# ConvNeXt block and Mamba block on one core: the down projection and the input projection put behind a sum on TensorE, and the depthwise convolution's parts put into other steps

## The chip, the cores and the metric

The kernel runs on one core of a Trainium2 chip. The metric is the device time of one execution in microseconds (us), taken as the median of several runs. A profile is one further execution, recorded instruction by instruction. Its engines are PE (TensorE, matrix products; PEld are its weight loads), DVE (VectorE), ACT (ScalarE), POOL (GpSimd) and SP, which only issues DMAs here.

## The reference

The input is 32 images of 96 channels and 56 x 56 pixels, in float32. Two layers follow each other.

Layer 0 is a ConvNeXt block: a depthwise 7 x 7 convolution, a norm over the channels, an up projection from 96 to 384 channels with Gelu, a down projection back to 96, and the residual.

Layer 1 takes the 3136 pixels of an image as a sequence and runs two Mamba blocks over it. Cut to what matters:

```python
xs, z = split(norm(seq) @ in_w)                 # 96 -> 2 x 192
xc = silu(conv4(xs) + conv_b)                   # causal, four taps
dt, Bm, Cm = split(xc @ xproj_w)                # 6, 16 and 16 columns
delta = softplus(dt @ dt_w + dt_b)              # 192
h[t] = exp(delta * A) * h[t-1] + delta * Bm * xc    # 192 x 16 states
y = (sum over the 16 states of h * Cm) + Dp * xc
seq = seq + (y * silu(z)) @ out_w
```

Then come a 1 x 1 fusion with a vector pooled from the layer's input, a batch norm over all images, and a residual.

## The kernel before, in words

**Stages.** One stage is one Mamba layer i of one image b for one quarter c of its sequence (784 positions, held as two halves of 392). There are 2 x 32 x 4 = 256 stages, listed in `order`, with layer 0 and layer 1 of the block alternating and a layer-1 stage standing two places behind the layer-0 stage of the same quarter. A stage has 24 steps: six groups j of 32 channels, times four groups g of four states. In each step `scan` runs one scan of 128 rows x 784 positions on VectorE (L885); the decay comes from ScalarE's exponential (`exps`, L836), and GpSimd multiplies the result by Cm (L889).

**The input of a scan.** For four of the six groups j, TensorE spreads u = delta * xc over the 128 rows (`spread`, L851, two matmuls into a "wide" PSUM tile of which there are two), and VectorE multiplies by Bm (L878) ahead of the scan. For the groups in `POOLED` (steps 8 to 11 and 20 to 23) GpSimd makes that product (L862), and the exponential goes into a wide tile. So a spread is issued in the steps 3, 11, 15 and 23, for the product that follows in step 4, 12, 16 and in step 0 of the next stage.

**The sums.** `add_up(n - 3)` in step n sums over the states with matmuls (L921) into the tile y, for odd j, behind a first matmul with D (L914) for g = 0. "The sums of step 15" are thus issued in step 18. `gate` (L903, VectorE) multiplies y by silu(z); there are three gates in a stage, in the steps 4 and 12 and behind the scan of step 19. The one behind step 19 reads the sums of steps 12 to 15.

**What lies between.** All other work is cut into pieces with a slot number. The whole part is the step (a negative number, or one over 24, lies in the stage before or after), the fraction orders the pieces of a step. In each step the order on every engine is: exponentials for later steps, the scan, the spread, the gate behind step 19, `add_up`, and then the pieces of that step.

- `prep`, for the stage that comes next: load, norm (`center` L355, `square` L360, `mean` L365, `root` L371), the input projection (`project`, L587: three blocks q of 64 columns with four taps, each in two pieces, into the PSUM tile of that q, then the z part), `silu` (L600), `dbl` (L614), `dt` (L644, 6 rows, all three PSUM tiles), `softplus` (L652), and the loads of Bm, Cm (`load_bc`), delta (`load_d4`) and u (`load_u`). The times t of the projection pieces apply to all stages but three special ones.
- `post`, for the stage that just ended: `project` at 7.5 (L750, L756), `move` at 9 and 10, and for layer 1 the statistics and the store.
- `block0`: half a quarter of the ConvNeXt block of the next image: norm, `up` (L424, the three PSUM tiles), `gelu` (L432), `down` (L439 and L443, PSUM tile 2), `residual` (L450, and a store on SP). At the end of an image come `total` (VectorE), `pool` (L464 on TensorE, Relu L466 on ScalarE) and `fuse` (L470, L472), both through PSUM tile 2.
- `conv`: the depthwise convolution of two channels for seven images, one per stage in the stages 2 to 145, as band matrices. Part 0 has four images, part 1 three; each has seven taps (L506, one matmul each), accumulated in PSUM tile 2, and a `store` (L519 on ScalarE, then a DMA). The band and the padded input are loaded at -1.

**Order on an engine.** The main part is under a manual schedule: each engine runs its instructions in the order of the program, and waits at the first that isn't ready. The PSUM tiles 0, 1 and 2 exist once each:

```python
return pp.tile([128, 512], F32, name="ps", tag=f"ps{k}", bufs=1)
```

so a piece that writes one of them waits until the last reader of what was in it is through. For each tile these readers are ScalarE or VectorE instructions.

Of the kernel before, what the change touches and what calls it, by code (L numbers as in the profile page):

```python
# [51 lines left out]
NCH = 4  # L52
# [9 lines left out]
def convnext_mamba_kernel(  # L62
# [185 lines left out]
    for k in range(2):  # L248
        t = const.tile([C + 1, 3 + CH], F32, name=f"hn{k}", tag=f"hn{k}")
        nc.vector.memset(t[C : C + 1, :], 1.0)  # L250
        hns.append(t)
        t = const.tile([C + 1, HC], F32, name=f"hz{k}", tag=f"hz{k}")
# [7 lines left out]
    with tc.tile_pool(name="cc", bufs=1) as cc, tc.tile_pool(name="cx", bufs=3) as cx, tc.tile_pool(  # L260
# [32 lines left out]
        for i in range(3):  # L293
            t = cc.tile([R2, 7, R2], F32, name=f"band{i}", tag=f"band{i}")
            nc.gpsimd.memset(t, 0.0)
            bands.append(t)
            t = cc.tile([R2, b0, W + 6], F32, name=f"xpad{i}", tag=f"xpad{i}")
# [31 lines left out]
    with ExitStack() as main:  # L329
# [23 lines left out]
        def centred(src, k):  # L353
            ps = psum(k)
            nc.tensor.matmul(ps[0:C, 0:HC], center_m, src, start=True, stop=True)  # L355
            return ps

        def squared(ps):
            sq = wp.tile([R2, HC], F32, name="sq", tag="sq", bufs=3)[0:C]
            nc.scalar.activation(sq, ps[0:C, 0:HC], AF.Square)  # L360
            return sq

        def mean_of(sq, k):
            ps = psum(k)
            nc.tensor.matmul(ps[0:C, 0:HC], mean_m, sq, start=True, stop=True)  # L365
            return ps

        def rsqrt(ps):

            rs = ps[0:C, 0:HC]  # L370
            nc.scalar.activation(rs, rs, AF.Ln, bias=eps_c[0:C])  # L371
            nc.scalar.activation(rs, rs, AF.Exp, scale=-0.5)
# [10 lines left out]
        def block0(b, c, s):  # L383
            k = c * 2 + s
            v = {}

            def load():
                if k == 0:
                    batch_sums[b] = wp.tile([C, NCH * 2], F32, name="sums", tag="sums", bufs=2)
                v["cv"] = wp.tile([C, ROWS, W], F32, name="cv", tag="cv", bufs=1)  # L390
                g = 0 if b < b0 else 1 + (b - b0) // NB
                at = (b - groups[g][0]) * W
                nc.sync.dma_start(
                    v["cv"],
                    conv_d[g].rearrange("(c h) w -> c h w", h=H)[
                        :, k * ROWS : (k + 1) * ROWS, at : at + W
                    ],
                )

            def load_x():  # L400
                if s == 0:
                    xins[b, c] = wp.tile([C, CH], F32, name="xin", tag="xin", bufs=1)
                    nc.sync.dma_start(xins[b, c], x[b, :, c * CH : (c + 1) * CH])

            def center():
                v["cv"] = v["cv"].rearrange("p r w -> p (r w)")
                v["ps"] = centred(v["cv"], 2)

            def square():
                v["sq"] = squared(v["ps"])  # L410

            def mean():
                v["ps"] = mean_of(v["sq"], 2)

            def root():
                rsqrt(v["ps"])

            def norm():
                nc.vector.tensor_tensor(hn0s[s][0:C], v["cv"], v["ps"][0:C, 0:HC], ALU.mult)

            def up():
                v["pss"] = [psum(f) for f in range(NF)]
                for f in range(NF):
                    nc.tensor.matmul(  # L424
                        v["pss"][f][:, 0:HC], w1_sb[:, f * 128 : (f + 1) * 128], hn0s[s],
                        start=True, stop=True,
                    )

            def gelu():
                v["gl"] = wp.tile([128, NF, HC], F32, name="gl", tag="gl", bufs=1)  # L430
                for f in range(NF):
                    nc.scalar.activation(  # L432
                        v["gl"][:, f], v["pss"][f][:, 0:HC], AF.Gelu, bias=b1_sb[:, f : f + 1]
                    )
                exp_ln_tables()

            def down():
                v["ps"] = psum(2)
                nc.tensor.matmul(  # L439
                    v["ps"][0:C, 0:HC], eye, xins[b, c][:, tok(s)], start=True, stop=False  # L440
                )
                for f in range(NF):
                    nc.tensor.matmul(  # L443
                        v["ps"][0:C, 0:HC], w2_sb[:, f, :], v["gl"][:, f, :],
                        start=False, stop=(f == NF - 1),
                    )

            def residual():
                xs = xins[b, c][:, tok(s)]
                nc.scalar.activation(  # L450
                    xs, v["ps"][0:C, 0:HC], AF.Identity, bias=b2ls,
                    accum_out=batch_sums[b][:, k : k + 1],
                )
                if s == 1:
                    nc.sync.dma_start(x1_d[b][:, c * CH : (c + 1) * CH], xins.pop((b, c)))


            def total():
                v["m"] = wp.tile([C, 1], F32, name="mean", tag="gps")
                nc.vector.tensor_reduce(v["m"], batch_sums[b], AX.X, ALU.add)  # L460

            def pool():
                ps = psum(2)
                nc.tensor.matmul(ps[0:C, 0:1], gpw_sb, v["m"], start=True, stop=True)  # L464
                v["gp"] = wp.tile([C, 1], F32, name="gp", tag="gps")
                nc.scalar.activation(v["gp"], ps[0:C, 0:1], AF.Relu, bias=gpb, scale=1.0 / L)  # L466

            def fuse():
                ps = psum(2)
                nc.tensor.matmul(ps[0:C, 0:1], fw2, v["gp"], start=True, stop=True)  # L470
                fb = wp.tile([C, 1], F32, name="fb", tag="fb", bufs=3)
                nc.scalar.activation(fb, ps[0:C, 0:1], AF.Identity, bias=fusb)  # L472
                batch_bias[b] = fb

            last = [(21.5, total), (29.9, pool), (30.9, fuse)] if k == 2 * NCH - 1 else []
            return last + [
                (-6, load), (2, load_x), (11.3, center), (12.1, square), (12.4, mean),
                (12.8, root), (14.1, True, norm), (15.6, up), (15.9, gelu), (17.3, down),
                (18.3, residual),
            ]  # L480


# [5 lines left out]
        def conv(g, p):  # L488
            lo, hi = groups[g]
            v = {}  # L490

            def load():
                v["band"] = wp.tile([R2, 7, R2], F32, name="band", tag="band", bufs=1)
                nc.sync.dma_start(v["band"].rearrange("p k n -> p (k n)"), band_d[p])
                nc.sync.dma_start(
                    xpad[:, :, 3 : 3 + W],
                    x[lo:hi, 2 * p : 2 * p + 2, :].rearrange("b c (h w) -> (c h) b w", w=W),
                )

            def tap(part, dw):  # L500
                first, last = PARTS[part]

                def piece():
                    if dw == 0:
                        v["ps"] = psum(2)
                    nc.tensor.matmul(  # L506
                        v["ps"][0:R2, 0 : (last - first) * W], v["band"][:, dw, :],
                        xpad[:, first:last, dw : dw + W], start=(dw == 0), stop=(dw == 6),
                    )

                return piece

            def store(part):
                first, last = PARTS[part]
                n = (last - first) * W

                def piece():
                    t = wp.tile([R2, HC], F32, name="sq", tag="sq", bufs=3)
                    nc.scalar.activation(  # L519
                        t[:, 0:n], v["ps"][0:R2, 0:n], AF.Identity, bias=cb[:, p : p + 1]  # L520
                    )
                    nc.sync.dma_start(
                        conv_d[g][p * R2 : (p + 1) * R2, first * W : last * W], t[:, 0:n]
                    )

                return piece

            at = (7.7, 8.2, 8.6, 9.2, 9.6, 10.2, 10.4), (18.5, 18.6, 19.2, 20.2, 21.2, 21.3, 22.2)
            return [
                (-1, load), (11.05, store(0)), (22.9, store(1)),  # L530
                *[(at[part][dw], tap(part, dw)) for part in range(2) for dw in range(7)],
            ]

# [7 lines left out]
        def prep(S):  # L541
# [164 lines left out]
                (-18, load), (-12.9, center), (-11.9, square), (-11.8, halo), (-11.6, mean),  # L706
                (-11.2, root), (-9, True, norm),
            ]
            t = (-7.6, -7.5, -6.5, -6, 0, 0.1, 1, 2.3, 3.1, 3.4, 4)
            if S in (stages[2], stages[-1]):  # L710

                start = [
# [3 lines left out]
                t = (12, 12, 13, 13, 14, 14, 15, 16, 17, 18, 19)  # L716
            elif S is stages[3]:
# [5 lines left out]
                t = (0, 0, 0.1, 0.2, 0.3, 1, 2, 3.3, 4.1, 4.4, 5)  # L723
            t = [k + 0.1 for k in t]
# [362 lines left out]
```

## Time and profile before

| what | value |
|---|---|
| median of 3 runs | 17,911.81 us (17,886.25 to 17,983.38) |
| the profiled execution | 17,900.79 us |
| its span from the first to the last instruction | 17,899.1 us |
| ahead of the first scan / from the last scan on | 639 us / 371 us |
| mean granted clock of TensorE | 0.851 |
| busy: VectorE, GpSimd, TensorE, ScalarE | 90%, 87%, 82%, 64% |
| TensorE's wait for VectorE's scans ahead of a spread (L851) | 2109.8 us |
| moved by DMA | 2346 MB, 131 GB/s |

Times in the table are from the runs and from the page of the profile. A row of the timeline or of the groups has, in this order, the start where it is a timeline, the time that the instructions took together, the engine, the line of the kernel, the operation, what it writes and reads, the shape (for matmuls rows x columns of the weights, then the moving operand) and the count; in brackets stand the idle time of the engine before it and who ended that. A row of waits has the waiting instruction, the one waited for, the time in total, how often, and the longest. A float32 matmul of the program stands as two instructions in the counts of TensorE.

### The profile page before, as it was taken

The numbers are of one execution on the slowest core, as the hardware profiler recorded it, in microseconds if no ns is written. First come the engines' busy times: TensorE is split into PE (matmuls) and PEld (weight loads), VectorE is DVE, ScalarE is ACT, GpSimd is POOL, SyncE is SP. The second block draws the span as 40 slices with busy tenths as digits, with TensorE's granted clock in tenths as the row PEclk, the third lists the DMA queues.
The fourth block names the chain that finished last, engine by engine and source line by source line (L and its number), as shares of the span: only waits on it lengthen the run. The fifth ranks groups of instructions, "written<-read, shape, count | busy, mean of one in ns | idle before, by whom it ended". The sixth has DMA issues, their size and how long they took to land.

```text
span 17899.1 us, 218250 instructions
## 1 busy us (share of the span) xinstructions
PE 14647.6 (82%) x67992; PEld 5293.3 (30%) x67992; DVE 16088.6 (90%) x12345; ACT 11435.6 (64%) x18647; POOL 15610.8 (87%) x8737
## 2 busy tenths in 40 slices
PE   7788888888888888888888888888888888888870
PEld 5233333333333333333333322222222222222220
DVE  7599999999999999999999999999999999999994
ACT  1566666666666666666666666666666666666653
POOL 0599999999999999999999999999999999999991
PEclk9788888888888888888888888888888888888885
DMA  4355555555555555555555545554545454554548
GB/s 102 90 137 131 136 130 137 135 134 137 132 136 136 135 135 134 131 136 132 136 132 133 134 120 125 122 125 122 123 121 125 121 125 121 124 124 120 125 111 275
DMA packets 1421987, 2346.49 MB, mean 131 GB/s; under 512 B 629958, under 2 KB 793586, under 8 KB 1420820
## 3 DMA queue, kind: packets, MB, share of 16 engines
q1 hardware_dynamic: 1413652, 2294.00, 52.4%
q10 hardware_dynamic: 7168, 38.54, 0.6%
q8 instruction: 536, 8.78, 0.2%
q14 instruction: 631, 5.17, 0.1%
HBM read 1929.11 MB, written 402.41 MB: 130 GB/s over the span
## 4 chain that ended last, share of the span: by engine, by line
PE 20%; DVE 18%; issue 4%; ACT 3%; DMA 3%; POOL 2%; SPq 0%; DVEq 0%; POOLq 0%; ACTq 0%
DVE h L885 14%; PE ps L587 5%; PE y L921 4%; DVE w L878 4%; PE w L851 3%; PE y L914 2%; PE ps L355 2%; PE ps L614 1%; ACT w L836 1%; POOL da L889 1%; PE ps L424 1%; DMA fr<-x_d 1%; POOL da L862 1%; PE ps L443 1%; DMA out_y<-fo 1%
## 5 line engine op out<-in xcount | busy, mean ns | idle before, releaser
L889 POOL TENSOR_TENSOR da<-h,bc 128x784 f32<-128x784 f32 x6144 | 11277.1, 1853 | 1301.0 <-DVE h L885 1187.5
L885 DVE TENSOR_TENSOR_SCAN h<-da,st,w 128x784 f32<-128x784 f32 x3072 | 5665.6, 1844 | 318.0 <-ACT st L896 8.2
L878 DVE TENSOR_TENSOR w<-w,bc 128x784 f32<-128x784 f32 x4096 | 3997.1, 976 | 550.4 <-PE w L851 394.0
L862 POOL TENSOR_TENSOR da<-us,bc 128x784 f32<-128x784 f32 x2048 | 3802.3, 1857 | 9.7 <-DMA us<-uu 9.7
L836 ACT ACTIVATE da<-d,A 128x784 f32<-128x784 f32 x4096 | 3756.9, 941 | 32.3 <-DMA d<-dd 18.5
L921 PE MATMUL y<-da,ssum 128*32 128x392 f32 x24576 | 3350.3, 577 | 237.8 <-POOL da L889 235.3
L836 ACT ACTIVATE w<-d,A 128x784 f32<-128x784 f32 x2048 | 1861.3, 915 | 2199.1 <-DVE h L885 2042.6
L851 PE MATMUL w<-u,sel 64*128 64x392 f32 x4096 | 1326.4, 733 | 2109.8 <-DVE h L885 2109.8
L885 DVE TENSOR_TENSOR_SCAN h<-w,st,da 128x784 f32<-128x784 f32 x1536 | 2712.5, 1827 | 3.4 <-POOL da L889 2.3
L587 PE MATMUL ps<-hn,wx 97*64 97x392 f32 x12288 | 2267.1, 503 | 14.9 <-DVE hn L575 14.9
L885 DVE TENSOR_TENSOR_SCAN h<-da,w 128x784 f32<-128x784 f32 x1024 | 1827.2, 1784 | 108.0 <-DVE w L878 2.9
L921 PEld LDWEIGHTS y<-da,ssum 128*32 128x32 f32 x24576 | 632.0, 117 | 2512.7 <-issue 1852.4
L587 PEld LDWEIGHTS ps<-hn,wx 97*64 97x64 f32 x12288 | 801.0, 137 | 1474.8 <-issue 1114.4
L666 POOL TENSOR_TENSOR u<-dl,xc 128x784 f32<-128x784 f32 (+1 forms) x512 | 738.3, 1442 | 560.7 <-ACT dl L652 560.7
L851 PEld LDWEIGHTS w<-u,sel 64*128 64x128 f32 x4096 | 409.1, 239 | 2700.8 <-DVE h L885 1539.6
L914 PE MATMUL y<-xc,D 128*128 128x392 f32 x1536 | 1141.6, 841 | 23.1 <-DVE z L903 23.1
L432 ACT ACTIVATE gl<-ps,b_sb 128x392 f32<-128x392 f32 x768 | 451.9, 588 | 1060.6 <-PE ps L424 1024.7
L351 ACT ACT_TABLE_LOAD x759 | 973.8, 1283 | 14.1 <-PEq L1074 0.8
L885 DVE TENSOR_TENSOR_SCAN h<-w,da 128x784 f32<-128x784 f32 x512 | 874.1, 1767 | 7.1 <-ACT w L836 7.1
L506 PE MATMUL ps<-xpad,band 112*112 112x224 f32 (+1 forms) x4032 | 856.9, 345 | 0.0
L600 ACT ACTIVATE xc<-ps,cb 128x392 f32<-128x392 f32 x768 | 423.9, 585 | 651.3 <-PE ps L587 648.3
L365 PE MATMUL ps<-sq,mean_m 96*96 96x392 f32 x1536 | 686.1, 580 | 149.6 <-ACT sq L360 149.6
(124 smaller groups left out, 15044.6 us busy)
## 6 DMA issues: line engine op xcount, KB each, us to landing
bc<-bd SPq DMA_DIRECT2D x4096, 196.0 KB, 4.7
d<-dd SPq DMA_DIRECT2D x6144, 98.0 KB, 3.5
us<-uu SPq DMA_DIRECT2D x2048, 98.0 KB, 2.2
dd<-dl SPq DMA_DIRECT2D x512, 294.0 KB, 3.8
uu<-u SPq DMA_DIRECT2D x1024, 49.0 KB, 2.3
band<-band_d SPq DMA_DIRECT2D x144, 343.0 KB, 5.4
cv<-conv_d SPq DMA_DIRECT2D x256, 147.0 KB, 2.5
xin<-in_x SPq DMA_DIRECT2D x128, 294.0 KB, 4.7
```

The costliest lines, as they stand in the source:

```text
L351: nc.scalar.preload_act_table_set("natural_log_exp_and_others")
L506: nc.tensor.matmul(v["ps"][0:R2, 0 : (last - first) * W], v["band"][:, dw, :], xpad[:, first:last, dw : dw + W], start=(dw == 0), stop=(dw ...
L587: nc.tensor.matmul(v["x", q][rows(a), 0:HC], weights[:, k, 64 * q : 64 * q + 64], v["hn"][:, o : o + HC], start=(k == 0), stop=(k == last),)
L666: nc.gpsimd.tensor_tensor(S.u[:, lo:hi], v["dl"][:, lo:hi], S.xc[:, lo:hi], ALU.mult)
L836: nc.scalar.activation(e, S.d4[j], AF.Exp, scale=S.d["A"][:, j, g : g + 1])
L851: nc.tensor.matmul(S.u4[:, 512 * a : 512 * a + HC], sel[rows(a), j % 2, :], S.u[rows(a), j // 2, :], start=True, stop=True,)
L862: nc.gpsimd.tensor_tensor(t, S.us[j], S.bcs[g][:, 0, :], ALU.mult)
L878: nc.vector.tensor_tensor(halves(db), S.u4.rearrange("p (a b) -> p a b", a=2)[:, :, 0:HC], halves(S.bcs[g][:, 0, :]), ALU.mult,)
L885: nc.vector.tensor_tensor_scan(ring[:, g, :], S.e.pop((j, g)), db, 0.0 if c == 0 else d["st"][:, j, g : g + 1], ALU.mult, ALU.add,)
L889: nc.gpsimd.tensor_tensor(da, ring[:, g, :], S.bcs[g][:, 1, :], ALU.mult)
L914: nc.tensor.matmul(S.y[:, 0:HC], S.d["D"][:, q, :], S.xc[:, q, :], start=True, stop=False)
L921: nc.tensor.matmul(S.y[r0 : r0 + 32, 0:HC], ssum, das[jj][:, tok(a)], start=False, stop=(g == NG - 1),)
```

## The change

It changes slot numbers alone; no instruction is added, removed or altered.

- `pool` goes from 29.9 to 28.85 and `fuse` from 30.9 to 29.1, that is from steps 5 and 6 of the following stage to steps 4 and 5.
- `down` goes from 17.3 to 18.2 and `residual` from 18.3 to 19.2.
- The taps of convolution part 0 go from steps 7 to 10 into the steps 5, 6, 7, 8 and 9, and its store from 11.05 to 10.05; the taps of part 1 go from steps 18 to 22 into the steps 20 to 22.
- The input projection's pieces for q = 0 and q = 1 go from 16.5, 16.6, 17.6 and 18.1 to 18.3, 18.4, 19.1 and 20.1 (t + 24 + 0.1). Those for q = 2 stay in step 0 of the stage itself.

```diff
@@ block0
-            last = [(21.5, total), (29.9, pool), (30.9, fuse)] if k == 2 * NCH - 1 else []
+            last = [(21.5, total), (28.85, pool), (29.1, fuse)] if k == 2 * NCH - 1 else []
             return last + [
                 (-6, load), (2, load_x), (11.3, center), (12.1, square), (12.4, mean),
-                (12.8, root), (14.1, True, norm), (15.6, up), (15.9, gelu), (17.3, down),
-                (18.3, residual),
+                (12.8, root), (14.1, True, norm), (15.6, up), (15.9, gelu), (18.2, down),
+                (19.2, residual),
             ]
@@ conv
-            at = (7.7, 8.2, 8.6, 9.2, 9.6, 10.2, 10.4), (18.5, 18.6, 19.2, 20.2, 21.2, 21.3, 22.2)
+            at = (5.5, 6.2, 6.6, 7.9, 8.5, 9.2, 9.6), (20.2, 20.3, 21.2, 21.3, 22.2, 22.3, 22.4)
             return [
-                (-1, load), (11.05, store(0)), (22.9, store(1)),
+                (-1, load), (10.05, store(0)), (22.9, store(1)),
                 *[(at[part][dw], tap(part, dw)) for part in range(2) for dw in range(7)],
             ]
@@ prep
-            t = (-7.6, -7.5, -6.5, -6, 0, 0.1, 1, 2.3, 3.1, 3.4, 4)
+            t = (-5.8, -5.7, -5, -4, 0, 0.1, 1, 2.3, 3.1, 3.4, 4)
```

## The prediction

> **What bounds the kernel now.** I read the page first, then VectorE's waits, then one stage in the timeline, then windows for the TensorE clock.
>
> ```profile
> PE 14647.6 (82%) x67992; PEld 5293.3 (30%) x67992; DVE 16088.6 (90%) x12345; ACT 11435.6 (64%) x18647; POOL 15610.8 (87%) x8737
> ```
>
> VectorE (DVE) is the busiest. A stage has 24 scans, 16 products, three gates and three norms there, and the 256 stages take 16,900 of the 17,899 us, some 66 us each. VectorE's own waits:
>
> ```profile
> DVE w L878 <- PE w L851: 394.0, 315, 8.6
> DVE z L903 <- PE y L921: 304.6, 249, 3.4
> ```
>
> So 700 us are VectorE standing for TensorE, at three places. I assigned VectorE's instructions of stages 6 to 249 to their steps: 1.09 us stand before the product of step 4 (spread issued in step 3), 0.47 before that of step 12, 1.22 before the gate behind step 19. 249 waits of 1.22 are the 304.6. Every other gap has a mean of at most 0.14.
>
> The gate in stage 101 (TensorE, then VectorE):
>
> ```profile
> 7329.78 0.87 PE L921 MATMUL y<-da,ssum 128*32 128x392 f32 x8
> 7330.57 2.86 PE L587 MATMUL ps<-hn,wx 97*64 97x392 f32 x16
> 7333.36 0.86 PE L921 MATMUL y<-da,ssum 128*32 128x392 f32 x8
> 7334.16 0.90 PE L439 MATMUL ps<-xin,eye 96*96 96x392 f32 x2
> 7334.89 2.14 PE L443 MATMUL ps<-gl,w_sb 128*96 128x392 f32 x6
> 7336.96 1.54 PE L587 MATMUL ps<-hn,wx 97*64 97x392 f32 x8
> 7338.43 0.87 PE L921 MATMUL y<-da,ssum 128*32 128x392 f32 x8
> 7339.23 1.54 PE L587 MATMUL ps<-hn,wx 97*64 97x392 f32 x8
> 7340.70 2.26 PE L506 MATMUL ps<-xpad,band 112*112 112x168 f32 x14
> 7345.34 1.68 PE L851 MATMUL w<-u,sel 64*128 64x392 f32 x4 [2.38 <-DVE h L885]
> ```
> ```profile
> 7336.39 1.85 DVE L885 TENSOR_TENSOR_SCAN h<-da,st,w 128x784 f32<-128x784 f32 x1
> 7339.39 0.57 DVE L903 TENSOR_TENSOR z<-y,z 128x392 f32<-128x392 f32 x1 [1.15 <-PE y L921]
> ```
>
> The scan of step 19 ends at 7338.24, but the sums of step 15 that the gate reads (7338.43) stand behind the down projection and three projection pieces. Only 3.7 us of TensorE work follow them, and then TensorE stands idle 2.38 us until scan 22 frees a buffer.
>
> The clock, in windows of 3.41 us from 7341.43 (elapsed, busy PE, PEld, DVE, ACT, POOL, granted clock, DMA):
>
> ```profile
> 7341.43:7344.84 3.41, 1.53 (x11) 1.26 (x9) 3.41 (x3) 2.27 (x3) 3.41 (x3) 1.00 0.43 118
> 7344.84:7348.25 3.41, 2.91 (x6) 1.03 (x6) 3.15 (x4) 3.39 (x6) 3.41 (x3) 0.50 0.84 209
> 7348.25:7351.67 3.42, 3.42 (x19) 0.90 (x20) 3.25 (x3) 2.20 (x3) 2.85 (x2) 0.50 1.07 246
> 7351.67:7355.08 3.41, 3.41 (x26) 1.02 (x22) 3.24 (x3) 0.59 (x1) 3.41 (x3) 1.00 1.03 236
> ```
>
> A window with 1.53 us busy is followed by half clock, and one that is busy throughout gives full clock back. Counted over the trace, each matmul weighted by its rows of 128: after all 520 full-clock windows under 0.3 the next was at half clock, after none of the 2481 over 0.5.
>
> **The change part by part.**
>
> *Down projection and projection pieces.* Nothing is added or removed; VectorE's and GpSimd's orders stay the same. TensorE's order becomes up, sums 13, 14, 15, down, projections q 0 and 1, taps. In stage 101 the up projection ends at 7329.78 and sums 13 to 15 take 3 x 0.80 (start to start), so y is complete at 7332.2; GpSimd's product of step 15 ended at 7328.4, so they need not wait for it. The gate is due at 7338.24: six us spare, more than the 1.8 that the worst stages now wait. The wait goes to zero: **-305 us**.
>
> What is late next? TensorE has the same work up to the spread of step 23: from 7332.2, 2.80 of down, 2.79 + 2.94 of projections and 2.26 of taps, to 7343.0; before it was 7342.96. Scan 22 ends 1.15 earlier, at 7344.05. So the spread still starts on time, with 1.1 us idle in place of 2.38. Over stages 4 to 249, the slack in front of this spread is at least 2.05 and the gate's wait at most 1.86, and stage by stage at least 0.2 is left. The residual on ScalarE now stands behind the exponential of step 20, which no longer waits for it; its bank is read (L450, 0.58) some 4 us before the taps need it. The store of x1 follows it on SP's queue: ahead of load_u in the same step as before, now behind store_u; its landing is needed more than a stage later. Cost nothing; were the 1.1 us of cover gone, each late microsecond of the spread would go straight to the next stage.
>
> *The clock behind the shorter idle time.* From scan 22 to the product of step 4, TensorE is a chain without a gap (spread, sums, projections, dbl, spread). I sorted the 142 stages 4 to 145 by the half-clock time in it: none in 66 stages, wait at step 4 0.10; 3.4 us in 52, 0.88; 6.8 us in 24, 2.17. With 1.2 us idle in a window and taps of 112 rows, the weighted activity is (3.41 - 1.2)/3.41 x 0.875 = 0.57, above the 0.5 that never led to half clock. Only stages whose gate wait is now near 0.5 keep some 1.8 us idle; I leave a tenth at half clock. The mean of 0.74 falls to about 0.2: 142 x 0.54 = **-77 us**. Bounds: 0 and 142 x 0.64 = -91. From stage 146 on there are no taps, the idle time goes from 4.5 to 3.3 us, some window is still mostly idle, and the wait at step 4 (1.56) stays, within 0.3 x 104 = 30 us either way.
>
> The Trainium skill ("TensorE: Matmul & The Clock Gate", Part 1: The HAM clock gate, and HAM oscillation) states that the clock falls after an idle window of about 3.4 us and gives "no PE-idle gaps >~3.4µs" as the rule; by it 2.38 us and 1.1 us are both harmless and this term is 0, the sum then 305 to 325. The window with 1.53 us busy speaks against it.
>
> *Conv taps at 5.5 to 9.6.* dt ends at time E (stage 101: 14.4 us into the stage). The first tap needs the third bank, which softplus (three of 0.586, behind the table load) leaves free only at E + 1.65; before, D of step 7 used this time. Behind the waiting tap stand D, sums 4 to 7, post's projection, and the spread of step 11. Work from there at full clock: taps 7 x 0.475, D 0.86, sums 4 x 0.80, post 3.63, together 11.0, then the spread's 0.93: E + 13.6 plus what half clock adds. dt (6 rows) and the wait make a low window, so half clock is sure; it ends after the first fully busy window behind E + 1.65, so it lasts 3.4 to 6.8 us and adds 1.7 to 3.4. That is E + 15.3 to 17.0. Scan 11 ends at E + 17.0 where step 4 did not wait, at E + 16.2 where it waited 0.8. So VectorE waits 0 to 0.8. Before, ordinary stages waited 0.36 on average (29 stages with 10.2 us of half clock 1.14, since sums 4 waited for GpSimd and broke the busy window). I take 0.2: 125 x 0.16 = **-20 us**; bounds -33 and +55. Band and padded input were issued 2.4 and 3.2 us into the stage and land by 10: no new wait. store(0) goes ahead of load_bc on SP and holds its eight DMAs some 3 us; they are for the next stage.
>
> *Pooling at 4.85 and 5.1.* In 17 stages with taps, pool waits for softplus and fuse for ScalarE's Relu, and VectorE waits 3.48 at step 12. After, fuse may start a microsecond earlier, but the first tap waits for its bias row behind an exponential, to about E + 4.4, where D stands now. The same work follows: 0, bounds -17 and +10.
>
> Sum: 305 + 77 + 20 = 402 us off the profiled execution's 17,900.8, that is 17,499; the median is 11 above that execution, so **17,510**.
>
> **Rivals.** (1) *Gate alone:* the clock between scan 22 and step 4 does not change, or what it gives is lost at step 12. For: the stages where the gate waits 0.46 stay near 2 us idle; also the page's rule. Against: windows and the three groups above. 17,911 - 305 = 17,600.
>
> (2) *Slower: the bank that the taps share.* The tap at 5.5 keeps the whole TensorE queue standing after dt, half clock lasts two windows longer than I allow, and every stage with taps waits at step 12 as the 17 pooling stages do. Price: 125 x (3.48 - 0.36) = 390, against 305 gained, so +85: 17,990. It decides from half clock of some 12 us in that stretch, or a 5 us wait for softplus. For: it is just what pooling does now. Against: softplus costs 1.65 there, and pooling stands 4.4.
>
> (3) *Given back:* TensorE, not VectorE, is the bound, and the spread of step 23 comes late by what the gate gained: 17,900. It would need negative slack, and the trace leaves 0.2 or more. The same time would come if the sums of step 15 were not earlier in effect, but they have six microseconds spare. GpSimd at 62.3 us of work a stage (32 x 1.855 + 2.9) would bind from 62.5 us a stage; I forecast 63.5 with taps and 64.9 without.
>
> **How the numbers follow.** Forecast 0.62 (own range 17,440 to 17,570), gate alone 0.22, partly given back (17,700 to 17,820) 0.04, given back whole 0.04, slower 0.08. The range is 17,430 to 17,680: its lower end takes the best bounds (305 + 91 + 33 + 17 + 30), its upper end the gate alone with 55 and 30 against it; some 0.17 lies outside. About 0.5%, 90 us, is what a measurement of this kernel can tell from no change: faster 0.88, same 0.04, slower 0.08.
>
> **What would show it.** Right: L903 waits under 20 us in all; L851's wait in front of step 24 near 1.2 us in stages with taps; the clock 1.00 there and L878 <- L851 down to some 300; mean clock up a little. Wrong: L903 still waiting over 100 us (sums not early), L878 waiting over 500 with ScalarE's softplus as releaser of the L506 weight loads (the bank), or a wait at step 0 (the spread late).

## The result, and the profile after

Four runs of the changed kernel have a median of 17,492.9 us (17,485.53 to 17,499.35), four of the kernel before 17,947.6 us (17,886.25 to 17,986.05): a ratio of 0.975, 95% interval 0.9716 to 0.9784. The forecast was 17,510. The profiled execution took 17,494.4 us, 406 less than the profiled one before. The median of the kernel before moves between 17,890 and 17,952 us from chip to chip, so each ratio below is against runs of it on the same chip. Two changed kernels are compared by their medians; where they may have run on different chips, the difference in the sum of the stages in their profiles (from the first scan of stage 0 to that of stage 255) stands beside.

The page:

```profile
PE 14220.3 (81%) x67992; PEld 5431.2 (31%) x67992; DVE 16065.8 (92%) x12345; ACT 11443.4 (65%) x18647; POOL 15590.5 (89%) x8737
```

VectorE's waits, longest first (only the first row is about TensorE):

```profile
DVE w L878 <- PE w L851: 280.9, 217, 8.5
DVE fo L1026 <- DMA fr<-x_d: 228.8, 64, 5.7
DVE hz L419 <- ACT ps L372: 126.5, 61, 16.4
```

The row of the gate, L903 <- L921 with 304.6 us, is gone from the list. Stage 101 in the timeline, TensorE and then VectorE:

```profile
7154.14 3.05 PE L424 MATMUL ps<-hz,w_sb 97*128 97x392 f32 x6
7157.11 2.18 PE L921 MATMUL y<-da,ssum 128*32 128x392 f32 x24
7159.23 0.90 PE L439 MATMUL ps<-xin,eye 96*96 96x392 f32 x2
7159.96 2.14 PE L443 MATMUL ps<-gl,w_sb 128*96 128x392 f32 x6
7162.03 5.50 PE L587 MATMUL ps<-hn,wx 97*64 97x392 f32 x32
7167.46 2.26 PE L506 MATMUL ps<-xpad,band 112*112 112x168 f32 x14
7170.74 0.93 PE L851 MATMUL w<-u,sel 64*128 64x392 f32 x4 [1.02 <-DVE h L885]
```
```profile
7163.05 1.85 DVE L885 TENSOR_TENSOR_SCAN h<-da,st,w 128x784 f32<-128x784 f32 x1
7164.81 0.54 DVE L903 TENSOR_TENSOR z<-y,z 128x392 f32<-128x392 f32 x1
```

The sums 13, 14 and 15 stand together behind the up projection and end at 7159.3, 5.5 us ahead of the gate. The gate follows its scan without idle time. The idle time ahead of the spread of step 23 is 1.02 in place of 2.38, and the spread takes 0.93 in place of 1.68: it runs at full clock. The windows of 3.41 us around it (elapsed, busy PE, PEld, DVE, ACT, POOL, granted clock, DMA):

```profile
7169.45:7172.86 3.41, 2.39 (x16) 0.83 (x18) 3.32 (x3) 3.41 (x6) 3.41 (x3) 1.00 0.43 130
7172.86:7176.27 3.41, 3.41 (x30) 1.27 (x24) 3.24 (x3) 2.98 (x4) 3.41 (x3) 1.00 1.06 241
```

By steps, as mean waits of VectorE in us (stages 4 to 145 have taps; 17 of them pool; 104 stages from 146 to 249 have none; "ordinary" stages have taps and do not pool). About 0.1 us stands ahead of a product that waits for nothing.

| wait | with taps, ordinary | pooling | without taps | us in all |
|---|---|---|---|---|
| gate behind step 19 | 1.17 to 0.00 | 1.47 to 0.00 | 1.23 to 0.00 | -301 |
| product of step 4 | 0.74 to 0.43 | 0.74 to 0.48 | 1.56 to 1.50 | -47 |
| product of step 12 | 0.36 to 0.12 | 3.48 to 2.11 | 0.10 to 0.10 | -53 |

The last column is the change of the mean over all 255 whole stages times 255; the three together are 401 of the 406 us.

### The profile page after: what moved, and what is told of

Its sections match the earlier page's. It is cut to its first block, busy times and chain, and to the rows that moved or that the text cites. A ratio compares the mean times of both kernels' runs of the same rounds, so it can differ in the third digit from the quotient of the medians.

```text
span 17492.7 us, 217908 instructions
## 1 busy us (share of the span) xinstructions
PE 14220.3 (81%) x67992; PEld 5431.2 (31%) x67992; DVE 16065.8 (92%) x12345; ACT 11443.4 (65%) x18647; POOL 15590.5 (89%) x8737
## 5 line engine op out<-in xcount | busy, mean ns | idle before, releaser
L885 DVE TENSOR_TENSOR_SCAN h<-da,st,w 128x784 f32<-128x784 f32 x3072 | 5664.1, 1844 | 317.6 <-ACT st L896 5.2
L836 ACT ACTIVATE da<-d,A 128x784 f32<-128x784 f32 x4096 | 3742.3, 941 | 31.1 <-DMA d<-dd 17.9
L836 ACT ACTIVATE w<-d,A 128x784 f32<-128x784 f32 x2048 | 1879.4, 918 | 2549.5 <-DVE h L885 2388.8
L921 PE MATMUL y<-da,ssum 128*32 128x392 f32 x24576 | 3077.7, 572 | 210.2 <-POOL da L889 208.7
L851 PE MATMUL w<-u,sel 64*128 64x392 f32 x4096 | 1281.5, 710 | 1982.0 <-DVE h L885 1980.2
L885 DVE TENSOR_TENSOR_SCAN h<-w,st,da 128x784 f32<-128x784 f32 x1536 | 2712.4, 1827 | 3.4 <-POOL da L889 2.3
L587 PE MATMUL ps<-hn,wx 97*64 97x392 f32 x12288 | 2153.0, 498 | 14.9 <-DVE hn L575 14.9
L885 DVE TENSOR_TENSOR_SCAN h<-da,w 128x784 f32<-128x784 f32 x1024 | 1826.9, 1784 | 112.6 <-ACT st L896 12.1
L921 PEld LDWEIGHTS y<-da,ssum 128*32 128x32 f32 x24576 | 668.1, 118 | 2242.8 <-issue 1763.4
L587 PEld LDWEIGHTS ps<-hn,wx 97*64 97x64 f32 x12288 | 842.2, 136 | 1321.3 <-issue 1126.3
L851 PEld LDWEIGHTS w<-u,sel 64*128 64x128 f32 x4096 | 398.8, 233 | 2624.4 <-DVE h L885 1600.5
L506 PE MATMUL ps<-xpad,band 112*112 112x224 f32 (+1 forms) x4032 | 1019.8, 393 | 206.5 <-ACT dl L652 194.6
L914 PE MATMUL y<-xc,D 128*128 128x392 f32 x1536 | 1091.6, 808 | 21.8 <-DVE z L903 21.8
L506 PEld LDWEIGHTS ps<-xpad,band 112*112 112x112 f32 x4032 | 691.2, 200 | 702.8 <-issue 322.7
L885 DVE TENSOR_TENSOR_SCAN h<-w,da 128x784 f32<-128x784 f32 x512 | 873.7, 1767 | 11.8 <-ACT w L836 11.8
```

What stands on the lines that cost most here:

```text
L506: nc.tensor.matmul(v["ps"][0:R2, 0 : (last - first) * W], v["band"][:, dw, :], xpad[:, first:last, dw : dw + W], start=(dw == 0), stop=(dw ...
L587: nc.tensor.matmul(v["x", q][rows(a), 0:HC], weights[:, k, 64 * q : 64 * q + 64], v["hn"][:, o : o + HC], start=(k == 0), stop=(k == last),)
L836: nc.scalar.activation(e, S.d4[j], AF.Exp, scale=S.d["A"][:, j, g : g + 1])
L851: nc.tensor.matmul(S.u4[:, 512 * a : 512 * a + HC], sel[rows(a), j % 2, :], S.u[rows(a), j // 2, :], start=True, stop=True,)
L885: nc.vector.tensor_tensor_scan(ring[:, g, :], S.e.pop((j, g)), db, 0.0 if c == 0 else d["st"][:, j, g : g + 1], ALU.mult, ALU.add,)
L914: nc.tensor.matmul(S.y[:, 0:HC], S.d["D"][:, q, :], S.xc[:, q, :], start=True, stop=False)
```

## The experiments

The theory on trial has two parts. The gate waited for what stood in TensorE's queue ahead of the sums of step 15. And the clock in TensorE's chain from the spread of step 23 to that of step 3 hangs on how idle it was just before. The rivals: the conv parts carry the gain, idle time is harmless, or what one wait gives another takes.

### Behind the sums alone

The kernel before, with (cut: `...` stands for what stays as it was)

```diff
-(17.3, down), (18.3, residual),
+(18.2, down), (19.2, residual),
-at = (...), (18.5, 18.6, 19.2, 20.2, 21.2, 21.3, 22.2)
+at = (...), (20.2, 20.3, 21.2, 21.3, 22.2, 22.3, 22.4)
-t = (-7.6, -7.5, -6.5, -6, 0, ...)
+t = (-5.8, -5.7, -5, -4, 0, ...)
```

> Only the down projection, its residual, the input projection's pieces and the taps of part 1 take their new slots; part 0, its store, pool and fuse stay at the old ones. Theory (the queue in front of the sums of step 15 is what the gate waits for): the gate's wait falls from 305 us to under 5, the wait at step 4 falls as in the changed kernel, since the idle time ahead of the spread of step 23 is the same, and the wait at step 12 stays as before (about 0.4 in ordinary stages with taps, 3.5 in the 17 pooling stages): 17,530 to 17,570 us. Rival (the conv parts carry the gain, by leaving TensorE free earlier): the gate still waits over 0.5 us a stage, 17,750 or more.

17,527.05 us, ratio 0.9763 (0.9748 to 0.9777), 3 us under the expected range. The gate waits 0.00, step 4 0.41 with taps, step 12 0.16 in ordinary stages (less than expected) and 3.18 in pooling stages. This part holds all but some 30 us of the gain (34 between the medians, 29 in the sum of the stages).

### Part 0 and pooling alone

The kernel before with the changed kernel's times for part 0, its store, pool and fuse.

> Only part 0 of the convolution with its store, pool and fuse take their new slots. Theory: the gate keeps its 305 us, the wait at step 12 falls to 0.1 to 0.2 in ordinary stages with taps and to about 2.1 in pooling stages, so 40 to 60 us below before. Rival (the earlier taps hold the queue at the softplus bank and cost time unless the rest of the change makes room): the wait at step 12 rises over 0.5 in ordinary stages, no gain or a loss of up to 50 us.

17,940.99 us, ratio 0.9994 (0.9984 to 1.0003): no gain that can be told, so the expectation failed. Step 12 did fall as expected (0.15 and 2.11), but step 4 rose from 0.74 to 1.19 in stages with taps, and the gate from 1.21 to 1.40. In the 106 stages with taps and about 2.4 us idle time ahead of the spread of step 23, half clock after that spread went from 2.16 us a stage to 4.22 on average. So the gain at step 12 went into the clock and the gate. The idle time itself is as before, 2.35 us on average, but it lies otherwise in the windows of 3.41 us in which the clock is granted. The trace shows that: call a window's activity its busy time, each matmul weighted by its rows of 128, as a share of the window. In both kernels half clock follows in the stages where the idle time leaves a window below an activity of about 0.41, and in none of the others: 47 of those 106 before, 87 here. What shifts the windows was not tested by itself.

### Each of the two moves by itself

e3_down_only is the first experiment without the edit of t; e4_proj_only is the edit of t alone.

> Down projection, residual and the taps of part 1 (they share the bank) take their new slots; the projection pieces stay in steps 16 to 18, two of the three blocks of four ahead of the sums of step 15. Theory: the sums come 2.8 us earlier, more than the longest wait of the gate (1.9), so the gate's wait is gone with this move alone: under 10 us in all, the time within 30 us of e1_behind_sums. Rival (the sums need both moves): the gate waits 0.3 to 0.9 us a stage.

> Only the input projection's pieces take their new slots; the down projection stays ahead of the sums of step 15. Theory: the sums come 4.3 us earlier, the gate's wait is under 10 us in all, the time within 40 us of e1_behind_sums. Rival (down is what holds the sums, because it waits for Gelu on ScalarE): the gate keeps over 0.5 us a stage.

The projection alone: 17,498.13 us, ratio 0.9746 (0.9727 to 0.9766), the gate at 0.00. The down projection alone: 18,055.21 us, ratio 1.0056 (1.0036 to 1.0076), slower than before, where a time within 30 us of the first experiment was expected. The gate waits 0.00, as expected, but VectorE has a new first row:

```profile
DVE h L885 <- ACT w L836: 476.2, 236, 2.8
DVE w L878 <- PE w L851: 370.6, 278, 9.5
```

Scans wait for exponentials. By steps it is scan 21, 1.96 us a stage. ScalarE's own waits say why:

```profile
ACT xin L450 <- PE ps L443: 1121.8, 256, 5.6
```

That row was 660.0 before. The projection pieces stay ahead of the moved down projection, so TensorE finishes it late (58.0 us into stage 29), and the residual, which waits for it, stands at 19.2 on ScalarE's queue ahead of the exponential of step 21. In the changed kernel the pieces go behind the down projection, which is done early.

### The residual out of the way

e3_down_only with

```diff
-(19.2, residual),
+(20.1, residual),
```

> e3_down_only with the residual at 20.1 in place of 19.2, behind the exponential of step 21 on ScalarE's queue. Theory (in e3_down_only the residual, waiting for a down projection that TensorE reaches late, held the exponential of step 21 and so scan 21): scan 21's wait of 2.0 us a stage is gone: 17,540 to 17,620 us. Rival (TensorE itself is late in that stretch): the time shows up as a wait at the gate or at step 0, 17,900 or more.

17,516.48 us, ratio 0.9759 (0.9739 to 0.9778), 24 us under the expected range. One slot number is worth 539 us here (544 in the sum of the stages): L885 <- L836 falls from 476 to 87 us, and the waits at step 4 fall, too (0.46 to 0.11 with taps, 1.84 to 1.02 without). So the down projection's move also suffices for the gate, if the residual does not hold ScalarE.

### Down projection put back

The changed kernel with down, residual and the taps of part 1 at their old times.

> The changed kernel with the down projection, its residual and the taps of part 1 put back to their old slots; the input projection, part 0, pool and fuse stay changed. Theory (moving the input projection behind the sums is the whole gain at the gate, the down projection's own move gives nothing, and part 0 gives its share at step 12 once the gate is gone): the gate's wait stays at zero, step 4 waits 0.1 with taps as in e4_proj_only, step 12 waits 0.1 to 0.15 in ordinary stages as in the changed kernel: 17,430 to 17,470 us. Rival (what step 12 gains from part 0 is given back at step 4, as in e2_part0_pool): 17,485 to 17,520.

17,431.98 us, ratio 0.9714 (0.9697 to 0.9730): faster than the changed kernel by 61 us (68 in the sum of the stages). The gate stays at 0.00. Step 4 waits 0.11 with taps, step 12 0.11 in ordinary stages and 1.90 in pooling stages. The down projection's move thus costs time here. With it put back, 0.81 us stay idle ahead of the spread of step 23 in the stages with taps, in place of 1.60, and none of them has half clock behind it. Part 0's earlier taps (with pool and fuse), worth nothing while the gate waited, are worth 66 us beside e4_proj_only (60 in the sum of the stages).

### Less work

The changed kernel with

```diff
-start=(dw == 0), stop=(dw == 6),
+start=(dw == 0), stop=(dw == 6 or part == 1),
-for part in range(2) for dw in range(7)
+for part in range(2) for dw in range(1 if part else 7)
```

> The changed kernel with one tap in place of seven in part 1 of the convolution: six matmuls of 0.32 us a stage are left out in stages 2 to 145 (that part of the output is not computed). TensorE's idle time ahead of the spread of step 23 grows from about 1.7 to 3.6 us there. Clock theory: the chain from scan 22 to step 4 then starts at half clock in all stages with taps, their wait at step 4 goes from 0.43 to about 1.5, and the kernel with less work is slower by 100 to 180 us: 17,590 to 17,670. Rival (the clock falls only after an idle window of 3.4 us or more, so the idle time is harmless; the shorter queue helps or does nothing): 17,440 to 17,500.

17,567.91 us, ratio 0.9819 (0.9805 to 0.9834): slower than the changed kernel by 75 us (by 72 in the sum of the stages) with 864 matmuls of the program left out, in the direction of the clock theory, though by less than it expected (100 to 180). The idle time became 2.5 to 4 us, and step 4 waits 0.89 with taps in place of 0.43, not 1.5. Of the 53 stages with about 3.5 us or more idle, all had half clock after the spread; of the 68 with about 3.0, 82%; of the 20 with about 2.5, four.

### Added work

The kernel before and the changed kernel with matmuls of no use ahead of the spread of step 23:

```diff
+        def fill(count):
+            def piece():
+                t = py.tile([128, 512], F32, name="y", tag="y")
+                for _ in range(count):
+                    nc.tensor.matmul(t[0:C, 0:FF], center_m, w1_sb[0:C], start=True, stop=True)
+            return piece
...
+            put(m, [(22.5, fill(2 if m < len(convs) + 2 else 5))])   # 3 and 8 on the kernel before
```

> The kernel before, with matmuls added ahead of the spread of step 23 whose result nobody reads (96 rows, 384 columns, into the y tile): three in the stages with taps, eight in the others, some 1.4 and 3.7 us. The gate is untouched. Clock theory: no half clock at the spread, the wait at step 4 goes from 0.74 to about 0.1 with taps and from 1.56 to about 0.2 without, the gate keeps its 305 us: 150 to 240 us below before. Rival (idle time is harmless): no gain, or a loss where a spread comes late.

> The changed kernel with the same added matmuls, two in the stages with taps and five in the others (some 0.95 and 2.3 us). Clock theory: the wait at step 4 goes from 0.43 to about 0.1 with taps and from 1.50 to about 0.2 without: 130 to 190 us below the changed kernel, 17,300 to 17,360. Rival (idle time is harmless): 17,490 or more.

On the kernel before: 17,656.96 us, ratio 0.9868 (0.9852 to 0.9885), 233 us faster with more work. Not one stage has half clock at that spread; step 4 waits 0.11 with taps and 0.12 without. The gate also fell, to 241.7 us, which had not been expected and whose cause is open:

```profile
DVE z L903 <- PE y L921: 241.7, 247, 4.2
DVE w L878 <- PE w L851: 169.2, 136, 8.5
```

On the changed kernel: 17,269.4 us, ratio 0.9652 (0.9637 to 0.9666), 31 us under the expected range. Step 4 waits 0.11 and 0.16, ordinary stages with taps wait 0.10 at step 12, and TensorE costs VectorE hardly anything:

```profile
DVE w L878 <- PE w L851: 63.7, 35, 8.6
```

This beats both kernels; the changed one by 224 us between the medians and 226 in the sum of the stages.

### Added work of six rows

The same with `center_m[0:6]` and `w1_sb[0:6]`.

> e7_fill_after with the added matmuls cut to 6 of 96 rows, the same count, columns and place, so TensorE is busy for about the same time. Theory (the clock follows busy time weighted by rows): they don't hold the clock, the wait at step 4 stays near 0.4 with taps and 1.5 without: 17,470 to 17,520 us. Rival (busy time alone holds the clock): 17,270 as with 96 rows.

17,441.19 us, ratio 0.9717 (0.9697 to 0.9736): 29 us under the expected range, but 172 us over the kernel with 96 rows (170 in the sum of the stages). Of the 104 stages without taps, 98 have half clock in the chain behind the spread of step 23 with six rows, 8 with 96. A stage without taps in windows of 3.41 us (elapsed, busy PE, PEld, DVE, ACT, POOL, granted clock, DMA), first with six rows:

```profile
13504.35:13507.76 3.41, 2.83 (x10) 1.25 (x10) 3.41 (x3) 2.59 (x4) 3.41 (x3) 1.00 0.46 120
13507.76:13511.17 3.41, 3.41 (x14) 0.90 (x14) 3.19 (x3) 3.39 (x4) 3.41 (x3) 0.50 0.80 175
13511.17:13514.59 3.42, 3.42 (x28) 1.18 (x20) 3.25 (x3) 1.11 (x3) 3.42 (x2) 1.00 1.05 240
```

and with 96 rows:

```profile
13397.40:13400.82 3.42, 3.08 (x12) 1.25 (x11) 3.42 (x3) 2.75 (x4) 3.42 (x3) 1.00 0.38 113
13400.82:13404.23 3.41, 3.41 (x26) 1.21 (x28) 3.19 (x3) 3.38 (x5) 3.41 (x3) 1.00 0.98 223
```

The added matmuls take the same time in the timelines of the two:

```profile
13503.32 3.46 PE L943 MATMUL y<-w_sb,center_m 6*96 6x384 f32 x10
```
```profile
13396.03 3.47 PE L943 MATMUL y<-w_sb,center_m 96*96 96x384 f32 x10
```

TensorE is busy 2.83 and 3.08 us of the window, yet the clock falls behind the first and stays behind the second. So the rows count, not busy time alone. The small difference in busy time is no rival: in the changed kernel (stages 4 to 249) half clock followed after 1 of the 181 full-clock windows that were 60 to 70% busy, and after 26 of the 2003 that were busy for 99% or more. Not all of the 172 us is this chain: with six rows the added matmuls themselves run at half clock in part in over a third of these stages, the spread is late, and step 0 waits 0.43 on average in place of 0.09, some 35 us over the 104. Part of the gain remains with six rows, since half clock is then shorter: in the 57 stages without taps and about 0.5 us idle it lasts 3.7 us on average, against 4.7 to 5.7 in most such stages of the changed kernel. What gives full clock back is a window that is busy almost throughout: in the changed kernel full clock followed after 640 of 689 half-clock windows that were at least 98% busy, and after none of 402 under 80%.

### Both together

e8_down_back with six such matmuls of 96 rows in the stages without taps alone.

> e8_down_back with six added matmuls of 96 rows ahead of the spread of step 23, in the stages without taps alone. Clock theory: the wait at step 4 of these 100 stages goes from about 1.25 to 0.15, 110 to 140 us below e8_down_back: 17,290 to 17,350 us, unless the stages with taps, too, start at half clock.

17,278.36 us, ratio 0.9627 (0.9613 to 0.9641), 154 us below e8_down_back and 12 us under the expected range; step 4 waits 0.11 everywhere. Its ratio and that of e7_fill_after overlap, so which of the two is the faster is open.

## Why the prediction was right, point by point

*The sum.* Forecast 402 us off the profiled execution, measured 406. That the two are so close is partly luck: the clock behind the spread of step 23 was taken 33 us too large, and part 0, pooling and the stages without taps 10, 23 and 6 us too small.

*The gate.* Forecast -305, measured -301. The sums come 5.5 us ahead of the gate where six were worked out. The runs add that either move alone frees the sums; nothing in the prediction said that the down projection's move is safe only because the projection moves behind it. It priced the residual's place on ScalarE at nothing, which holds with the projection moved and fails without (e3_down_only).

*The spread of step 23 stays on time.* Right: the least slack in front of it in stages 4 to 249 is 0.61 us.

*The clock.* The mechanism was right (fill, six rows and left-out taps all move step 4 with the half clock), the size was not: forecast -77 in the stages with taps, measured -44. The step that failed is "TensorE has the same work up to the spread", read as the same time, and with it 1.2 us idle and a tenth of the stages at half clock. VectorE's stretch from scan 14 to scan 22 did shrink by 1.31 us (22.40 to 21.09), but TensorE's stretch from the spread of step 15 to the last tap shrank as well, by 0.57 (20.15 to 19.58). So 1.60 us stay idle on average, and half clock stands behind the spread in 49 of the 141 stages 4 to 144, a third and not a tenth. Of the 51 stages with about 2.0 us idle 47 have it, of the 28 with about 1.5 one, of the 48 with about 1.0 none. The length alone does not decide: of the 14 with about 2.5 us only one has it. In the other 13 the idle time is split over two windows and neither falls below an activity of 0.42; in the 47 the lowest window has 0.31 to 0.41.

The 0.57 can be read from the timeline: matmuls of one kind that stand together take less. The three groups of sums take 2.18 where one takes 0.87, the projections 5.50 where the pieces took 2.86 and twice 1.54. On average over the stages with taps, from start to start, the sums of this stretch take 3.45 in place of 3.78 and the projections 5.42 in place of 5.73; half clock in it is the same, 4.9 us.

*Part 0.* Forecast -20 in ordinary stages with 0.2 left, measured -30 with 0.12. The wait at the bank is there as worked out, 1.56 us a stage, and off VectorE's path:

```profile
PE ps L506 <- ACT dl L652: 194.6, 125, 1.7
```

Half clock in that stretch, 10.2 us in 29 ordinary stages before, is 3.4 or 6.8 in all of them after. That this part gives nothing while the gate still waits (e2_part0_pool) is a case that the prediction did not look at.

*Pooling.* Forecast 0, measured -23 at step 12. The first tap starts 4.2 us behind dt, where 4.4 was worked out. Wrong was "the same work follows". In stage 50, post's projection (L756) and the spread of step 11 (L851), before and after:

```profile
3962.11 3.95 PE L756 MATMUL ps<-z,ow 64*96 64x392 f32 x12
3971.79 0.93 PE L851 MATMUL w<-u,sel 64*128 64x392 f32 x4
```
```profile
3873.26 2.22 PE L756 MATMUL ps<-z,ow 64*96 64x392 f32 x12
3879.87 0.93 PE L851 MATMUL w<-u,sel 64*128 64x392 f32 x4
```

From the end of the one to the start of the other it is 5.73 us in all 17 stages before and 4.40 after: all seven taps stood between them, now four do. Scan 11 hangs on the same projection, because ScalarE moves its result (L764) ahead of the exponential of step 11:

```profile
3966.10 0.49 ACT L764 ACTIVATE seq<-ps 96x392 f32<-96x392 f32 x1 [2.18 <-PE ps L756]
3966.49 0.91 ACT L836 ACTIVATE w<-d,A 128x784 f32<-128x784 f32 x1
```

So the wait behind scan 11 falls by the same 1.33 us, from 3.48 in all 17 stages to 2.15 in 15 of them. The clock is not what did it: in ten of the 17 half clock lasts 10.2 us before and after. Some of the gain is given back ahead of scan 11, whose own wait for its exponential goes from 0.42 to 0.70 us, 5 us in all.

*The stages without taps.* Forecast 0 within 30, measured -6 at step 4.

*Rivals.* Gate alone: the wait at step 4, which goes with the clock, gave 47 us, so no. The bank: no wait of that size. Given back: not in the change. In e2_part0_pool and e3_down_only a gain is given back, but to the clock and to ScalarE's queue, not by a late spread of step 23. As for the rule of the Trainium skill ("TensorE: Matmul & The Clock Gate", Part 1: The HAM clock gate) that the clock falls after an idle window of about 3.4 us, the runs do not agree: with six rows it fell behind a window that was busy 2.83 of 3.41 us.

## What to carry to other kernels

Where one engine's queue feeds the engine that sets the time, order each step by when its result is due, and check the reader of every moved result as well: its place in its own queue can turn the saved wait into a longer one elsewhere. Before removing idle time or work ahead of a TensorE chain, look at the granted clock in windows, since the length of the idle time alone did not tell it here; here matmuls of no use, with many rows, in that idle time were worth 224 us. A gain that has room at one wait may only show once the next wait is gone: measure parts together as well as alone.

## What the runs showed of the hardware that had not been expected

- The fall of TensorE's clock goes by rows as well as by time: ten instructions of 3.46 us in all with 6 rows do not hold it, ten of 3.47 us with 96 rows do.
- Weighting busy time by rows of 128, no full-clock window over 0.5 was followed by half clock in stages 4 to 249 of the kernel before and the changed one (some 2500 windows each) and that with fill (some 2800). Under 0.3 the fall was certain before (520 of 520), but not after: 15 of some 535 windows kept full clock, and 23 of some 445 with fill.
- In the changed kernel 2.5 us of idle time ahead of the chain left the clock full in the 13 of 14 stages in which it was split over two windows with enough work in each, while 2.0 us in one window halved it in 31 of 32.
- Three groups of 32-column sums in a row take 2.18 us, where one by itself takes 0.87.
